# Projecting q, k and v of a slice in one place with full-size matmuls, in a four-layer attention and convolution kernel

## The chip, the cores and the metric

The kernel runs on one core of one Trainium2 chip. The metric is the device time of one execution in microseconds (us); the lower, the better. A core has a matmul engine (TensorE, PE in the profile; its weight loads are PEld), a vector engine (VectorE, DVE), an engine for functions and evictions (ScalarE, ACT), a general engine (GpSimd, POOL) and an engine that here only issues transfers (SyncE, SP).

## The reference

The input x is 4 images of 256 channels and 48 x 48 points, in float32. Four layers follow, each of the form x = x + layer(group norm of x):

- Layer 0: `qkv = w_qkv @ x`; q and k of each of 8 heads (64 channels) are divided by their norm over the 2304 points; `softmax(10 * q^T k)` weighs v; `w_out` projects the result.
- Layer 1: maximum pooling, a blur with stride 3, four depthwise convolutions of 11 x 3, a sigmoid gate that is spread back over the points and multiplies the layer's input.
- Layer 2: theta, phi and g project 256 channels to 64; `softmax(theta phi / 8)` over the 2304 points weighs g; `W` projects back to 256; a normalization over all images.
- Layer 3: a gate for each channel from the mean over the points, a depthwise 3 x 3 convolution, a normalization over the points and a leaky relu.

The change is in the projections of layers 0 and 2:

```python
qkv = jnp.einsum('oc,bchw->bohw', w_qkv, x)                    # layer 0
theta_x = jnp.einsum('oc,bcn->bno', theta_w, xt) + theta_b     # layer 2
phi_x = jnp.einsum('oc,bcn->bon', phi_w, xt) + phi_b[:, None]
g_x = jnp.einsum('oc,bcn->bno', g_w, xt) + g_b
```

## The kernel before

All four images stay in on-chip memory, as X[b], 128 partitions x 2 halves of the channels x 2304 points. The group norm is not applied to x: its scale goes into the weights (`norms`, L462) and its shift into a bias.

**Units, groups and slots.** Layer 0 goes through 16 phases, one for each image and pair of heads. A phase has six units (`l0_unit`, 384 query points each), and a unit has nine groups of two key blocks of 128 points. One group is one slot, so that a phase has 54. In a slot, `attend` writes out by hand, in this order: `scores` of the group (L239, quarter matmuls of 64x64, then exp on ACT into pt, L245), `add_up` of the group before (the sums for the softmax, on DVE into acc, L285, for some groups after a first addition on POOL into half, L270), what is due in the slot, the fills of the slot, the steps of layer 1 (`others`), and `weigh` of the group before (L259, into av). Every engine works through its own instructions in the order written. pt has five buffers, the PSUM tiles sc and pj two each.

**The end of a unit.** When its last group is weighed, in slot 0 of the next unit, `last` books: in slot 1 `total` (L292, the column sums of acc, into both pj tiles), in slot 4 `invert`, in slot 8 `divide`, and eleven slots later, in slot 2 of the unit after next, `out_proj`: two matmuls (L527) and two additions to X on DVE (L531).

**The next pair.** While a phase attends one pair of heads, it projects q, k and v of the next, slice by slice (384 points, read again from memory into xs, two buffers). `start` in slot 0 loads the weights w, `norms` in slot 2 scales them and makes a bias. `qk` stands in slots 4 and 6 of each unit: for each of two halves of the channels it issues four quarter matmuls (`quarters`, L226) into two pj tiles, one for each half of the rows, and `join` brings the first to q or k on ACT with the bias (L229), and adds the second on DVE (L230). Then ACT squares it for the norm (junk, L489). `values` (L497, full matmuls of 128x128) stands in slot 2 of the next unit, ahead of out_proj; the last slice's comes in the next phase (`late`). `scale` in slot 51 multiplies all of q (L518). For the first pair the same functions run one after another before `attend`.

**Layer 1 and layer 2.** Layer 1 of an image is cut into steps, mainly of DVE (L643 is its largest group), which run in the slots of the next image's phases. Image 0's phases have none. Layer 2 has three units for each image, of two column halves at once: kd holds phi twice, qv theta of one half of the points above theta of the other. `project2` of the next image is spread over slots, as phi (L703), theta (L714, one half of the columns in one call) and g (L727) for each slice; phi and theta are joined as q and k are. Layer 3 comes last.

In the hardware's count every float32 matmul is two instructions.

Of the kernel before, what the change touches and what calls it, by code (L numbers as in the profile page):

```python
# [9 lines left out]
F32 = mybir.dt.float32  # L10
# [4 lines left out]
P = 128  # L15
HW = 48
N = HW * HW
NK = 2
# [56 lines left out]
def usual_path(  # L75
# [146 lines left out]
    def quarters(outs, lhsT, rhs, start, stop):  # L222

        for c in HALVES:
            for r, out in zip(HALVES, outs):
                nc.tensor.matmul(out[c], lhsT=lhsT[r, c], rhs=rhs[r], start=start, stop=stop)  # L226

    def join(out, ab, bias):
        nc.scalar.activation(out, ab[0], AF.Identity, bias=bias)  # L229
        nc.vector.tensor_add(out, ab[1], out)  # L230

# [197 lines left out]
    def project(b, norm, pair):  # L429
# [9 lines left out]
        def start():  # L439
            at["w"] = wqp.tile([P, NK, 3, P], F32, tag="w", name="w")  # L440
            for k in range(NK):
                nc.sync.dma_start(at["w"][:, k], wqv[:, k, :, p * P : (p + 1) * P])
            fetch(0)
            pair["q"] = big.tile([P, N], F32, tag="q", name="q")
            pair["k"] = big.tile([P, N], F32, tag="k", name="k")
            pair["v"] = big.tile([P, JB, P], F32, tag="v", name="v")
            at["ss"] = small.tile([P, 2, NSL], F32, tag="ss", name="ss")

        def norms():

            w = at["w"]
            ps = pj_tile()
            for t in range(3):
                for k in range(NK):
                    nc.tensor.matmul(
                        ps[:, t : t + 1], lhsT=w[:, k, t, :], rhs=norm["nb"][:, k : k + 1],
                        start=k == 0, stop=k == NK - 1,
                    )
            at["bias"] = small.tile([P, 3], F32, tag="bias", name="bias")
            nc.vector.tensor_copy(at["bias"], ps[:, 0:3])  # L460
            for k in range(NK):
                nc.scalar.activation(  # L462
                    w[:, k], w[:, k], AF.Identity, scale=norm["rs"][:, k : k + 1]
                )
            fetch(1)
# [15 lines left out]
        def qk(s, t):  # L481
            cols = slice(s * SL, (s + 1) * SL)
            to = pair["qk"[t]]
            ab = [pj_tile()[:, :SL] for _ in range(2)]
            for k in range(NK):
                quarters(ab, at["w"][:, k, t, :], xs[s][:, k, :], k == 0, k == NK - 1)
            join(to[:, cols], ab, at["bias"][:, t : t + 1])
            junk = rpool.tile([P, SL], mybir.dt.bfloat16, tag="junk", name="junk")
            nc.scalar.activation(  # L489
                junk, to[:, cols], AF.Square, accum_out=at["ss"][:, t, s : s + 1]  # L490
            )

        def values(s):
            ps = pj_tile()
            for i in range(SL // P):
                for k in range(NK):
                    nc.tensor.matmul(  # L497
                        ps[:, i * P : (i + 1) * P], lhsT=xs[s][:, k, i * P : (i + 1) * P],
                        rhs=at["w"][:, k, 2, :], start=k == 0, stop=k == NK - 1,
                    )  # L500
            j0 = s * (SL // P)
            nc.scalar.copy(
                pair["v"][:, j0 : j0 + SL // P, :].rearrange("p j d -> p (j d)"), ps[:, :SL]
            )
            if s + 2 < NCH:
                fetch(s + 2)

        def scale():
# [9 lines left out]
            nc.vector.tensor_scalar(pair["q"], pair["q"], sc, None, ALU.mult)  # L518

        return start, norms, out_bias, qk, values, scale  # L520
# [149 lines left out]
    def project2(b, norm, s2):  # L670
# [3 lines left out]
        def start():  # L674
# [15 lines left out]
            w = wqp.tile([P, NK, 3, P], F32, tag="w", name="w2")  # L690
            for k in range(NK):
                nc.scalar.activation(
                    w[:, k, :, 0:D], w2c[:, k], AF.Identity, scale=norm["rs"][:, k : k + 1]
                )
            at["w"], at["bias"] = w, bias

        def phi(s):
            cols = slice(s * SL, (s + 1) * SL)
            ab = [pj_tile()[:, :SL] for _ in range(2)]
            for k in range(NK):  # L700
                for c in HALVES:
                    for r, out in zip(HALVES, ab):
                        nc.tensor.matmul(  # L703
                            out[c], lhsT=at["w"][r, k, 0, 0:D], rhs=X[b][r, k, cols],
                            start=k == 0, stop=k == NK - 1,
                        )
            join(s2["k"][:, cols], ab, at["bias"][:, 0:1])

        def theta(s):
            c, to = HALVES[s // L2C], (s % L2C) * SL  # L710
            ab = [pj_tile()[:, :SL] for _ in range(2)]
            for k in range(NK):
                for r, out in zip(HALVES, ab):
                    nc.tensor.matmul(  # L714
                        out[c], lhsT=at["w"][r, k, 1, 0:D],
                        rhs=X[b][r, k, s * SL : (s + 1) * SL],
                        start=k == 0, stop=k == NK - 1,
                    )
            join(s2["q"][c, to : to + SL], [half[c] for half in ab], at["bias"][c, 1:2])

        def g(s):
            ps = pj_tile()
            nj = SL // P
            for i in range(nj):
                for k in range(NK):
# [3 lines left out]
                        rhs=at["w"][:, k, 2, 0:D], start=k == 0, stop=k == NK - 1,  # L729
# [5 lines left out]

        return [start] + [
            (lambda fn=fn, s=s: fn(s)) for s in range(NCH) for fn in (phi, theta, g)
        ]

# [59 lines left out]
    order = [(b, p) for b in range(B) for p in range(NPAIR)]  # L799
    n = NCH * NG  # L800
    late = None
    for (b, p), after in zip(order, order[1:] + [None]):
        work, others = {}, []
        if late:
            work[2] = [late]
        if after:
            b1, p1 = after
            start, norms, out_bias, qk, values, scale = project(b1, norms0[b1], pairs[b1][p1])
            work.setdefault(0, []).append(start)
            work.setdefault(2, []).append(norms)  # L810
            work[NG + 2] = [out_bias]
            for s in range(NCH):
                for t, slot in ((0, 4), (1, 6)):
                    slot += NG * s - (s == NCH - 1)
                    work.setdefault(slot, []).append(lambda qk=qk, s=s, t=t: qk(s, t))
                if s + 1 < NCH:
                    work.setdefault(NG * (s + 1) + 2, []).append(lambda v=values, s=s: v(s))
            work.setdefault(n - 3, []).append(scale)
            late = lambda v=values: v(NCH - 1)
# [35 lines left out]

    _drain(gn(0, norms0[0]))
    start, norms, out_bias, qk, values, scale = project(0, norms0[0], pairs[0][0])
    start()
    norms()
    for s in range(NCH):  # L860
        for t in range(2):
            qk(s, t)
        values(s)
    scale()
    out_bias()
# [1128 lines left out]
```

## Time and profile before

| | |
|---|---|
| median of 3 runs | 3950.24 us (3950.04 to 3954.59) |
| the profiled execution | 3949.85 us, span 3948.0 us |
| PE busy | 3614.1 us, 92% |
| DVE busy | 2939.9 us, 74% |
| ACT busy | 2089.8 us, 53% |
| POOL busy | 1449.4 us, 37% |
| first scores of layer 0 | 70.29 us after the span's start |
| layer 0 to about 3140 us, layer 2 to about 3660 us, then layer 3 | |

The page gives the busy time of each engine, the same in 40 slices of 98.7 us as tenths, and groups of equal instructions with their mean duration. An engine's idle time is put down to the instruction that ended it (`<-`). Matmuls overlap, so that the time from one start to the next, which the timeline shows, is what a matmul costs in a row, and its own duration (485 ns here) is longer. The quarter matmuls run four at a time.

### The profile page before, as it was taken

How to read it: one execution, taken by the hardware profiler on the slowest of the kernel's cores; microseconds unless marked ns; L12 is line 12 of the kernel's file. 1: busy time of each engine (PE TensorE's matmuls, PEld its weight loads, DVE VectorE, ACT ScalarE, POOL GpSimd, SP SyncE). 2: the span in 40 equal slices, each digit the busy share in tenths (PEclk: the TensorE clock that was granted, in tenths of full speed). 3: DMA queues.
4: the chain of work that ended last, by engine and by line, in shares of the span. 5: the costliest groups of instructions: out<-in, count | busy, mean ns of one | idle time of the engine just before them, and what ended most of it. 6: DMA issues, size and time to landing. Idle time of an engine off the chain costs nothing.

```text
span 3948.0 us, 91093 instructions
## 1 busy us (share of the span) xinstructions
PE 3614.1 (92%) x38738; PEld 1751.8 (44%) x38738; DVE 2939.9 (74%) x3733; ACT 2089.8 (53%) x3226; POOL 1449.4 (37%) x858
## 2 busy tenths in 40 slices
PE   6999999999999999999999999999999988779785
PEld 3444444444444444444444444444444444334343
DVE  2566555678987896789878967897788678856477
ACT  3666656655555555565565555655655544334222
POOL 1333333333333333333433333334334355443232
PEclk9999999999999999999999999999999999889787
DMA  4111111111111111111111111111110000000001
GB/s 148 24 25 21 24 20 29 24 20 24 20 24 20 24 20 24 24 24 20 21 20 26 20 24 20 24 20 23 21 13 8 6 5 5 5 5 4 0 36 61
DMA packets 109439, 91.09 MB, mean 23 GB/s; under 512 B 56048, under 2 KB 106848, under 8 KB 107104
## 3 DMA queue, kind: packets, MB, share of 16 engines
q1 hardware_dynamic: 106256, 84.06, 12.0%
q8 instruction: 305, 5.00, 0.5%
q10 hardware_dynamic: 2768, 1.14, 0.1%
q14 instruction: 110, 0.90, 0.1%
HBM read 54.62 MB, written 9.44 MB: 16 GB/s over the span
## 4 chain that ended last, share of the span: by engine, by line
PE 57%; DVE 30%; issue 5%; ACT 4%; POOL 3%; DMA 1%; SPq 0%; DVEq 0%; ACTq 0%; POOLq 0%
PE av L259 19%; PE sc L239 18%; DVE acc L285 14%; DVE l1acc L643 6%; PE pj L226 6%; PE pj L527 3%; PE pj L497 3%; PE sc L1028 3%; PE pj L292 2%; POOL half L270 1%; ACT pt L245 1%; DVE gn_st L168 1%; ACT k L229 1%; DVE k L230 1%; DVE z L1043 1%
## 5 line engine op out<-in xcount | busy, mean ns | idle before, releaser
L245 ACT ACTIVATE pt<-sc 128x768 f32<-128x768 f32 x1944 | 1482.4, 809 | 1096.2 <-PE sc L239 934.9
L270 POOL TENSOR_TENSOR half<-pt 128x768 f32<-128x768 f32 x477 | 977.5, 2050 | 2105.4 <-ACT pt L245 1893.6
L239 PE MATMUL sc<-q,k 64*64 64x384 f32 x13824 | 1288.6, 485 | 17.7 <-ACT pt L245 15.2
L259 PE MATMUL av<-pt,v 64*64 64x384 f32 x13824 | 1299.9, 489 | 4.7 <-ACT raw L328 4.7
L285 DVE TENSOR_TENSOR acc<-acc,pt 128x768 f32<-128x768 f32 x792 | 943.9, 1192 | 62.5 <-ACT pt L245 1.9
L239 PEld LDWEIGHTS sc<-q,k 64*64 64x64 f32 x13824 | 527.2, 134 | 625.8 <-issue 523.0
L259 PEld LDWEIGHTS av<-pt,v 64*64 64x64 f32 x13824 | 522.0, 134 | 611.3 <-issue 596.0
L285 DVE TENSOR_TENSOR acc<-acc,half 128x768 f32<-128x768 f32 x459 | 480.7, 1047 | 68.7 <-POOL half L270 65.7
L643 DVE SCALAR_TENSOR_TENSOR l1acc<-pd,grid,l1acc 128x256 f32<-128x256 f32 x640 | 464.4, 726 | 16.3
L531 DVE SCALAR_TENSOR_TENSOR x<-pj,bo,x 128x384 f32<-128x384 f32 x192 | 118.5, 618 | 263.3 <-PE pj L527 262.9
L226 PE MATMUL pj<-xs,w 64*64 64x384 f32 x3072 | 290.7, 485 | 5.7 <-ACT q L229 4.1
L239 PE MATMUL sc<-qv,kd 64*64 64x384 f32 x1728 | 188.8, 504 | 18.3 <-ACT pt L245 18.2
L259 PE MATMUL av<-pt,qv 64*64 64x384 f32 x1728 | 197.7, 522 | 6.3 <-ACT raw L328 6.3
L292 PE MATMUL pj<-acc,ones 64*64 64x384 f32 x832 | 98.4, 534 | 99.5 <-DVE acc L285 98.6
L1028 PE MATMUL sc<-pad,diag 128*128 128x384 f32 x480 | 173.4, 516 | 11.9 <-ACT pad L1006 11.9
L226 PEld LDWEIGHTS pj<-xs,w 64*64 64x64 f32 x3072 | 118.3, 133 | 142.5 <-issue 125.7
L527 PE MATMUL pj<-o,wo 128*128 128x384 f32 x384 | 158.9, 518 | 16.7 <-DVE bias L460 11.1
L497 PEld LDWEIGHTS pj<-w,xs 128*128 128x128 f32 x1152 | 135.9, 191 | 53.5 <-issue 42.8
L497 PE MATMUL pj<-w,xs 128*128 128x128 f32 x1152 | 153.8, 283 | 4.0 <-ACT k L229 4.0
L230 DVE TENSOR_TENSOR k<-pj,k 128x384 f32<-128x384 f32 x96 | 53.4, 556 | 138.1 <-ACT k L229 136.1
L336 POOL TENSOR_TENSOR o<-o,rinv 128x384 f32<-128x384 f32 x95 | 138.9, 1462 | 0.0
L230 DVE TENSOR_TENSOR q<-pj,q 128x384 f32<-128x384 f32 x96 | 53.5, 557 | 112.0 <-ACT q L229 112.0
(190 smaller groups left out, 2654.3 us busy)
## 6 DMA issues: line engine op xcount, KB each, us to landing
xs<-in_x_dram SPq DMA_DIRECT2D x96, 384.0 KB, 3.2
rinv<-rinv SPq DMA_DIRECT2D x208, 94.5 KB
x<-in_x_dram SPq DMA_DIRECT2D x8, 1152.0 KB, 5.4
out_dram<-x SPq DMA_DIRECT2D x7, 1152.0 KB, 4.2
l<-row SPq DMA_DIRECT2D x416, 1.5 KB, 1.8
w<-in_wqkv_dram SPq DMA_DIRECT2D x32, 192.0 KB, 6.7
rinv<-ls SPq DMA_DIRECT2D x208, 1.5 KB, 1.8
out_dram<-x SPq DMA_DIRECT2D x2, 576.0 KB, 3.3
```

The costliest lines, as they stand in the source:

```text
L226: nc.tensor.matmul(out[c], lhsT=lhsT[r, c], rhs=rhs[r], start=start, stop=stop)
L230: nc.vector.tensor_add(out, ab[1], out)
L239: nc.tensor.matmul(ps[c * D : (c + 1) * D, h, :SL], lhsT=u["of"]["k"][r, j0 : j0 + D], rhs=u["of"]["q"][r, u["qc"]], start=True, stop=True,)
L245: nc.scalar.activation(pt, ps[:, :, :SL], AF.Exp, scale=u["scale"])
L259: nc.tensor.matmul(u["av"][h * D : (h + 1) * D, half, :SL], lhsT=value(u, j, h)[r], rhs=pt[r, h, :], start=j == 0, stop=j == JB - 1,)
L270: nc.gpsimd.tensor_add(half, pts[0], pts[1])
L285: nc.vector.tensor_add(u["acc"], u["acc"], term)
L292: nc.tensor.matmul(out[c], lhsT=ones[r], rhs=u["acc"][r, h, :], start=True, stop=True)
L497: nc.tensor.matmul(ps[:, i * P : (i + 1) * P], lhsT=xs[s][:, k, i * P : (i + 1) * P], rhs=at["w"][:, k, 2, :], start=k == 0, stop=k == NK - 1,
L527: nc.tensor.matmul(ps[:, :SL], lhsT=wo[:, p, k * P : (k + 1) * P], rhs=o, start=True, stop=True)
L643: nc.vector.scalar_tensor_tensor(acc, src, w, acc, ALU.mult, ALU.add)
L1028: nc.tensor.matmul(self.ps[:, s % 2, :SL].rearrange("p (r c) -> p r c", c=HW), lhsT=diag[:, self.k, PE_TAPS.index(t), :], rhs=self.pad[:, ...
```

## The change

q, k and v of a slice are now made by one function, `chunk`, in slot 2 of each unit, ahead of out_proj: `values`, then q, then k. q and k are full matmuls, 128 rows and 128 columns, accumulated over the two halves of the channels in one pj tile; ACT brings them to q and k with the bias, and DVE has no part in it. `quarters` and `join` are gone. The weights are loaded half a phase earlier (`prefetch`, slot 27 of the phase before) and scaled in slot 47 of the phase before (`norms`), `start` reads the first two slices, `scale` multiplies q in three parts in slots 51 to 53, and nothing is late. In layer 2 phi's weights are stored twice, side by side, so that one full matmul gives both copies of kd; theta makes both halves of the columns in one call, as two matmuls of 128 rows and 64 columns, in three calls and not six.

```diff
-    def quarters(outs, lhsT, rhs, start, stop):
-
-        for c in HALVES:
-            for r, out in zip(HALVES, outs):
-                nc.tensor.matmul(out[c], lhsT=lhsT[r, c], rhs=rhs[r], start=start, stop=stop)
-
-    def join(out, ab, bias):
-        nc.scalar.activation(out, ab[0], AF.Identity, bias=bias)
-        nc.vector.tensor_add(out, ab[1], out)
...
-        def start():
+        def prefetch():
             at["w"] = wqp.tile([P, NK, 3, P], F32, tag="w", name="w")
             for k in range(NK):
                 nc.sync.dma_start(at["w"][:, k], wqv[:, k, :, p * P : (p + 1) * P])
-            fetch(0)
-            pair["q"] = big.tile([P, N], F32, tag="q", name="q")
...
+        def start():
+            pair["q"] = big.tile([P, N], F32, tag="q", name="q")
...
+            fetch(0)
             fetch(1)
...
         def qk(s, t):
             cols = slice(s * SL, (s + 1) * SL)
-            to = pair["qk"[t]]
-            ab = [pj_tile()[:, :SL] for _ in range(2)]
+            to = pair["qk"[t]][:, cols]
+            ps = pj_tile()[:, :SL]
             for k in range(NK):
-                quarters(ab, at["w"][:, k, t, :], xs[s][:, k, :], k == 0, k == NK - 1)
-            join(to[:, cols], ab, at["bias"][:, t : t + 1])
+                nc.tensor.matmul(
+                    ps, lhsT=at["w"][:, k, t, :], rhs=xs[s][:, k, :],
+                    start=k == 0, stop=k == NK - 1,
+                )
+            nc.scalar.activation(to, ps, AF.Identity, bias=at["bias"][:, t : t + 1])
...
+        def chunk(s):
+            values(s)
+            for t in range(2):
+                qk(s, t)
             if s + 2 < NCH:
                 fetch(s + 2)
...
-            nc.vector.tensor_scalar(pair["q"], pair["q"], sc, None, ALU.mult)
+            at["sc"] = sc
+            rescale(0)
+
+        def rescale(i):
+            q = pair["q"][:, i * 2 * SL : (i + 1) * 2 * SL]
+            nc.vector.tensor_scalar(q, q, at["sc"], None, ALU.mult)
...
         def phi(s):
+
             cols = slice(s * SL, (s + 1) * SL)
-            ab = [pj_tile()[:, :SL] for _ in range(2)]
+            ps = pj_tile()[:, :SL]
             for k in range(NK):
...
+                nc.tensor.matmul(
+                    ps, lhsT=at["w"][:, k, 0:2, :].rearrange("p t d -> p (t d)"),
+                    rhs=X[b][:, k, cols], start=k == 0, stop=k == NK - 1,
+                )
+            nc.scalar.activation(
+                s2["k"][:, cols], ps, AF.Identity, bias=at["bias"][:, 0:1]
+            )
 
         def theta(s):
...
+            ps = pj_tile()[:, :SL]
             for k in range(NK):
-                for r, out in zip(HALVES, ab):
+                for i, c in enumerate(HALVES):
+                    s0 = (s + i * L2C) * SL
                     nc.tensor.matmul(
...
+                        ps[c], lhsT=at["w"][:, k, 2, :], rhs=X[b][:, k, s0 : s0 + SL],
                         start=k == 0, stop=k == NK - 1,
                     )
...
+            new = projs[i + 1]
+            work[0] = [new["start"]]
             for s in range(NCH):
...
+                work[NG * s + AT_CHUNK] = [lambda new=new, s=s: new["chunk"](s)]
+            work[NG + AT_CHUNK].append(new["out_bias"])
+            for j, fn in enumerate(new["scale"]):
+                work[n - 3 + j] = [fn]
+            if i + 2 < len(order):
+                work[n // 2] = [projs[i + 2]["prefetch"]]
+                work[NG * (NCH - 1) + AT_CHUNK].append(projs[i + 2]["norms"])
```

## The prediction, made before the changed kernel ran

> **What bounds the kernel now.** I read first the slices of the page, then windows of busy time, then the waits of VectorE (DVE) and TensorE (PE), then the timeline of the start and of one unit. The slices:
>
> ```profile
> PE   6999999999999999999999999999999988779785
> DVE  2566555678987896789878967897788678856477
> ```
>
> PE is full from slice 2 to about 32, and not in the first or in layer 2 and 3. DVE rises and falls: low while image 0 is attended, high where layer 1 of an earlier image rides along. Two windows (sum, then PE, PEld, DVE, ACT, POOL, clock, DMA) give sizes:
>
> ```profile
> 400.00:700.00 300.00, 298.60 (x3457) 146.39 (x3450) 175.41 (x223) 180.15 (x282) 101.55 (x63) 1.00 0.15 24
> 1000.00:1300.00 300.00, 280.26 (x3156) 132.93 (x3152) 253.99 (x311) 169.76 (x271) 113.81 (x63) 0.98 0.13 21
> ```
>
> In the first PE idles 1.4 us of 300, in the second 19.7, with DVE at 85%. Who waits:
>
> ```profile
> DVE x L531 <- PE pj L527: 262.9, 172, 7.0
> DVE k L230 <- ACT k L229: 136.1, 60, 3.6
> DVE q L230 <- ACT q L229: 112.0, 88, 5.1
> PE pj L292 <- DVE acc L285: 98.6, 65, 6.5
> ```
>
> The last is what DVE costs PE: at the end of a unit the sums of acc are late and total (L292) waits. The first is DVE waiting for the output projection, in the middle of its own queue. One unit shows both:
>
> ```profile
> 1015.25 0.88 PE L292 MATMUL pj<-acc,ones 64*64 64x384 f32 x8 [1.40 <-DVE acc L285]
> 1019.11 1.58 PE L497 MATMUL pj<-w,xs 128*128 128x128 f32 x12
> 1020.53 1.64 PE L527 MATMUL pj<-o,wo 128*128 128x384 f32 x4
> 1021.38 0.62 DVE L531 SCALAR_TENSOR_TENSOR x<-pj,bo,x 128x384 f32<-128x384 f32 x1 [1.57 <-PE pj L527]
> ```
>
> From total to total a unit takes 29.6 us with image 0, which is PE's own work, and 31 to 35 us with layer 1 beside it. So there the loop is: acc done, PE to the output projection, DVE from there to the next acc. The start is a chain of single steps:
>
> ```profile
> 34.25 0.58 ACT L229 ACTIVATE q<-pj,bias 128x384 f32<-128x384 f32 x1 [1.61 <-PE pj L226]
> 34.86 0.56 DVE L230 TENSOR_TENSOR q<-pj,q 128x384 f32<-128x384 f32 x1 [3.80 <-ACT q L229]
> 34.88 2.11 PE L226 MATMUL pj<-xs,w 64*64 64x384 f32 x16 [0.68 <-ACT q L229]
> ```
>
> Both pj buffers belong to one q or k, so PE stops for each: 7.14 us a slice (L226 at 32.05 and 39.20), first scores at 70.29.
>
> **What the Trainium skill says.** "TensorEngine Tiling (Array Packing)", Key Properties: a change of tiling mode drains TensorE. The trace agrees: starts of matmul groups are 0.32 us apart inside one mode, 0.41 to 0.42 at a change. "TensorE: Matmul & The Clock Gate", queue depths under its architectural detail: ScalarE and VectorE are strict first-in first-out. The waits at L531 agree: additions ready behind it don't overtake. "SBUF — State Buffer", shared port: a DVE instruction with two SBUF inputs and a GpSimd one exclude each other. The trace agrees in size: an acc addition takes 0.95 us alone and up to 2.5 us beside half (2.05 us).
>
> **The change, part by part.**
>
> (1) *Full instead of quarter matmuls for q and k.* Sixteen quarter instructions (L226, 1002.07 to the next group at 1003.36) take 1.29 us of PE. Four full ones: L1028, the same 128x384 shape, issues 20 in 6.72 us, (6.72 - 0.485)/19 = 0.33 us each, 1.3 us. Its weight loads (0.19 us) hide behind that. So nothing changes: 0. Price if they didn't hide: L527 also shows 0.43 us; 4 x 0.1 x 192 = 80 us, taken as a tail only. Layer 2's phi is the same exchange, eight quarters for two full ones in a slice; its doubled weights are two small copies on ScalarE (ACT, busy 53%) ahead of the first use. Mode changes stay one pair a unit, because chunk sits in slot 2 with out_proj, where values were.
>
> (2) *No joins.* 96 q and 96 k at 0.556 us: 107 us less on DVE, 1.11 us a unit. The 0.62 us for which ACT waits before each junk goes too. Only beside layer 1 is DVE late, so for image 0 I take 0 (PE's 29.6 us hide it).
>
> (3) *chunk ahead of out_proj.* q and k were at slots 4 and 6; now 2 x 1.29 = 2.58 us stand in slot 2 ahead of out_proj, whose result L531 waits for in DVE's queue. Behind L531 stand the unit's layer 1 step and four rounds of acc additions. From total to the first L531 is 5.7 us in most units; it becomes 8.3, while DVE comes there at 4.4. PE has 2.58 us less to do afterwards, so the loop gains 2.58 of wait and loses 1.11 of joins and 0.35 of their wait: about +1.1 us where DVE is busy all the way, and I add 0.1 for additions that fall beside half. By the unit-to-unit timeline that holds in about 36 units; in 28 others with layer 1 DVE waits for q or k anyway, so the late end is set by PE's slots: -1.0 to +0.8, I take -0.3. 36 x 1.2 - 28 x 0.3 = **+35 us**. Bounds: 0 (the waits at L230 were all on the path) and +96 (64 x 1.5, none was).
>
> (4) *Start.* A slice is 1.34 us of values and 2.58 of q and k, 3.94 with the mode alike; ACT needs 0.48 + 2 x (0.58 + 0.71), 3.1, and each pj tile is free before PE returns to it. Six: 23.6 from 24.2, so 47.8. Then k's eviction and square 1.5, the scale chain 1.5, a third of the q rescale (1.42/3) 0.5: scores at 51.3, 19.0 earlier. Given back: x of images 1 to 3 (6 x 1152 KB) is issued at about 41 and moves at the 421 GB/s of before's 60 to 65 us, until 57.5; xs of the next pair stands behind it on SP's queue and lands at about 59.5, while chunk in slot 2 wants it at 57.2. Net **-16.5** (-19 to -12).
>
> (5) *Prefetch, norms, rescale.* w comes half a phase early, norms moves to slot 47, behind chunk and ahead of out_proj; the same 12 matmuls and the same copy by DVE ahead of L531. SP's order changes only by DMAs that wait for nothing late. In the last unit the sums of squares are ready four slots before scale (L510 and L515 waited 1.5 us). Chunk makes out_proj's second tile wait for k's eviction by 0.1 us. On ACT the chunk queues three evictions and two squares, 3.1 us, between the exps of slots 2 and 3; PE needs 6.5 us from the first to the second (1.34 + 2.58 + 1.3 + 1.29 of L259), so the exps aren't late; the cover is gone if an exp of slot 2 itself waits over 1 us for DVE to free its pt, and then out_proj waits for both. The xs reads of a slice are issued behind chunk and wanted nine slots later, so their 3.2 us are hidden; v of the new pair is first written in slot 2 and not in slot 11, after the last reading of the old one in slot 0. **-1** (-6 to +6).
>
> (6) *Last phase of layer 0.* project2 for image 0: theta halves. L714's eight instructions use two of four quarters, 1.29 us a slice for six slices; after, three calls of 1.29, if two 128x64 tiles run together, which L344 shows (pairs start 6 ns apart). -3.9 on PE; 12 joins leave DVE, and no chunk is added here: **-9** (-12 to -3).
>
> (7) *Layer 2.* In 3200 to 3400 DVE is busy 171.5 of 200 us and PE 161.6, so DVE's 24 joins (kd, qv, 13.3 us) and 4 of their waits come off the path: -16. In image 2's last unit (about 3497 to 3570) project2 is a chain as at the start: PE waits 0.8 for ACT kd in each slice, 4 for DVE kd, 1.6 more, and theta's 3.9: -12. **-28** (-40 to -15).
>
> Sum against the profiled execution, 3949.85 us (span 3948.0 and 1.85 around it): +35 - 16.5 - 1 - 9 - 28 = -19.5, **3930 us**. The median of the runs is 3950.24, 0.4 above it, so they stand for the same.
>
> **Rivals.** A change of 0.2%, 8 us, is about what a measurement here can tell.
>
> *L531 blocks more than the joins free* (slower). Mechanism as in (3), in all 64 units at 1.5 us: +96 - 54.5 = +41, **3991 us**. For it: DVE comes to L531 at 4.4 us, so it would sit idle for 4 us a unit; heavy layer 1 steps and half can't be moved into that hole. Against: 28 units had waits at L230 of 1.6 us and more. It decides once the mean loss passes 54.5/64 = 0.85 us a unit, and is over 0.2% from 0.97.
>
> *DVE's relief is paid in full* (faster). The waits at L230 (248 us) were on the path, so (3) is 0: **3895 us**. For it: the chain of waits runs through L230 beside layer 1. Against: where DVE is late, that wait is only 0.35 us.
>
> *The full matmuls issue at 0.43 us*: +80 us, about 4010. Against it stand 20 in a row at 0.33.
>
> **How the numbers follow.** Forecast 0.50 (its own range 3905 to 3955), L531 slower 0.31, relief in full 0.15, slow issue 0.04. The forecast's cases fall 0.37 faster, 0.10 same, 0.03 slower; the relief's are all faster; those of L531 start near the break-even, 0.03 of them within 0.2%. Faster 0.52, same 0.13, slower 0.35. The range, 3885 to 3990, reaches to both first rivals.
>
> **What will show it.** First scores near 51 us. q and k without DVE; PE L478 at 1.3 us for four. DVE's wait at out_proj's addition up from 263 us to over 450; units beside layer 1 at 32 to 36 us, PE's wait for acc at total up from 99 us to 120 or more. Three calls of theta at 1.3 us. Layer 2 ended 28 us sooner after its start. If the wait at the addition stays at 263 us, (3) is wrong; if total's wait falls, the relief won; if units grow by over 1 us on the mean, the first rival has.

## The result and the profile after

The changed kernel takes **3969.5 us** (median of 4 runs, 3967.5 to 3976.9) where the kernel before takes 3950.1 on the same chip: a ratio of 1.0050, with a 95% interval of 1.0032 to 1.0067. It is half a per cent slower; 3930 us, faster, was forecast. The profiled execution is the longest of the four runs, 3976.9 us with a span of 3975.0, 7.4 us above the median, so the two profiles are 27 us apart and not 19: the differences between their stages below carry up to 7 us that the other executions did not have.

The slices of the changed kernel's page (busy tenths of PE and DVE):

```profile
PE   7999999999899999999899999998999997879785
DVE  2565555568888787678787876887878769966477
```

PE is fuller at the start and emptier while layer 1 rides along: slices 11, 20 and 28 fall to 8, while DVE there is mostly below what it was. Neither engine is busier there, and the kernel is slower. The same two windows as before (length, then busy us of PE, PEld, DVE, ACT, POOL, granted clock, DMA share, GB/s):

```profile
400.00:700.00 300.00, 296.44 (x3210) 147.42 (x3210) 169.65 (x208) 178.98 (x279) 96.88 (x63) 1.00 0.15 25
1000.00:1300.00 300.00, 272.42 (x2813) 132.20 (x2806) 240.89 (x278) 165.77 (x262) 109.23 (x61) 0.98 0.13 21
```

In the second, PE idles 27.6 us of 300 (19.7 before) and DVE has 13 us less to do. Both wait more. The waits say for what (total us, times, longest):

```profile
DVE x L539 <- PE pj L535: 398.2, 153, 9.1
...
ACT pt L235 <- DVE acc L275: 154.3, 152, 4.4
...
PE pj L282 <- DVE acc L275: 127.0, 63, 7.5
...
DVE bias L445 <- PE pj L440: 99.1, 15, 10.0
...
DVE bo L470 <- PE pj L462: 72.7, 12, 8.4
```

The addition of out_proj (L539, L531 before) waits 398 us and not 263, total 127 and not 99. The copies of the norms' bias and of bo, which stand behind the chunk as well, wait 172 us together (69.7 before). The 248 us of waits at the joins are gone with them; the new waits at these three places, 237 us, nearly fill their place. Exp (L235) waits 154 us for acc to give back a pt tile, where it waited 46. The unit shown of the kernel before at 1015.25 is this one now (timeline of the changed kernel, PE and DVE):

```profile
1016.07 0.88 PE L282 MATMUL pj<-acc,ones 64*64 64x384 f32 x8 [1.74 <-DVE acc L275]
...
1019.46 1.60 PE L492 MATMUL pj<-w,xs 128*128 128x128 f32 x12
...
1020.90 2.75 PE L478 MATMUL pj<-xs,w 128*128 128x384 f32 x8
1023.48 0.50 PE L462 MATMUL pj<-bias,wo 128*128 128x1 f32 x4
1024.02 0.16 DVE L470 COPY bo<-pj 128x2 f32<-128x2 f32 x1 [3.46 <-PE pj L462]
1024.33 1.53 PE L535 MATMUL pj<-o,wo 128*128 128x384 f32 x4 [0.34 <-DVE bo L470]
1025.25 1.26 DVE L539 SCALAR_TENSOR_TENSOR x<-pj,bo,x 128x384 f32<-128x384 f32 x2 [1.07 <-PE pj L535]
```

From total to the addition it was 6.1 us; it is 9.2, and DVE stands idle for 3.46 + 1.07 us of it. The start is shorter: first scores at 53.12 us, not 70.29. But:

```profile
53.12 1.52 PE L229 MATMUL sc<-q,k 64*64 64x384 f32 x16 [1.17 <-DVE q L523]
...
65.50 2.90 PE L492 MATMUL pj<-w,xs 128*128 128x128 f32 x12 [6.42 <-DMA xs<-in_x_dram]
```

The first chunk of the loop waits 6.42 us for its xs, and PE's next starts are at half pace (12 instructions of L492 took 1.6 us above and take 2.9 here). The clock that was granted to TensorE, in the column before the last two, is 0.50 there:

```profile
65.50:68.50 3.00, 3.00 (x13) 3.00 (x14) 0.00 (x0) 0.06 (x1) 0.00 (x0) 0.50 0.06 18
```

For everything that follows the span is cut at the totals into six stages, worked out from the starts of total (first of its eight matmuls): to the first total; image 0 (24 units); the 65 units beside layer 1; the last phase of layer 0, up to the first total of layer 2; layer 2, up to its last total; the rest.

| profile of | start | image 0 | beside layer 1 | last phase | layer 2 | rest |
|---|---|---|---|---|---|---|
| before | 100.9 | 720.7 | 2116.2 | 226.0 | 406.7 | 377.5 |
| changed | 91.8 | 725.6 | 2181.1 | 221.0 | 375.7 | 379.9 |
| difference | -9.1 | +4.9 | **+64.9** | -5.0 | **-31.0** | +2.4 |

By the place of a unit in its phase, the 65 units split. The four kinds of unit without the phase's last chunk (44 units) lost 34.6 us together, 0.8 us each. The 11 that hold the last chunk, norms and scale lost 35.5 us, 3.2 us each; the remaining 10, which begin a phase and held norms in the kernel before, gained 5.3 together.

One thing differs between executions as well. In image 0 the granted clock never falls. Beside layer 1 the trace's record of it has stretches at 0.50, each 3.4 or 6.8 us long, and in these two profiles each follows an idle gap of PE of 1.9 to 4.8 us: 14 stretches, 54.6 us, before, and 16, 71.7 us, in the changed kernel. At half the clock PE does half its work, so a stretch costs at most half its length, and by this estimate at most 9 of the 64.9 us are the clock's. The waits come first.

### The profile page after: what moved, and what is told of

It reads as the page before. It is cut to its first block, busy times and chain, and to the rows that moved or that the text cites. A ratio compares the mean times of both kernels' runs of the same rounds, so it can differ in the third digit from the quotient of the medians.

```text
span 3975.0 us, 85528 instructions
## 1 busy us (share of the span) xinstructions
PE 3601.6 (91%) x36050; PEld 1764.9 (44%) x36050; DVE 2862.1 (72%) x3525; ACT 2092.1 (53%) x3222; POOL 1421.2 (36%) x858
## 4 chain that ended last, share of the span: by engine, by line
PE 50%; DVE 39%; issue 5%; ACT 3%; POOL 2%; DMA 1%; DVEq 0%; SPq 0%; ACTq 0%; POOLq 0%
DVE acc L275 21%; PE av L249 15%; PE sc L229 14%; DVE l1acc L651 8%; PE pj L478 6%; PE pj L535 4%; PE pj L492 3%; PE sc L1041 3%; PE pj L282 2%; ACT pt L235 1%; DVE z L1056 1%; DVE x L675 1%; DVE gn_st L168 1%; DVE lsum L312 1%; PE pj L740 1%
## 5 line engine op out<-in xcount | busy, mean ns | idle before, releaser
L235 ACT ACTIVATE pt<-sc 128x768 f32<-128x768 f32 x1944 | 1492.4, 810 | 1263.7 <-PE sc L229 1000.4
L260 POOL TENSOR_TENSOR half<-pt 128x768 f32<-128x768 f32 x477 | 952.5, 1998 | 2173.8 <-ACT pt L235 1710.3
L275 DVE TENSOR_TENSOR acc<-acc,pt 128x768 f32<-128x768 f32 x792 | 970.4, 1225 | 86.4 <-DVE acc L275 3.2
L275 DVE TENSOR_TENSOR acc<-acc,half 128x768 f32<-128x768 f32 x459 | 497.7, 1084 | 166.3 <-POOL half L260 163.9
L651 DVE SCALAR_TENSOR_TENSOR l1acc<-pd,grid,l1acc 128x256 f32<-128x256 f32 x640 | 451.7, 706 | 16.2
L539 DVE SCALAR_TENSOR_TENSOR x<-pj,bo,x 128x384 f32<-128x384 f32 x192 | 118.3, 617 | 399.1 <-PE pj L535 398.2
L478 PE MATMUL pj<-xs,w 128*128 128x384 f32 x768 | 268.1, 490 | 9.9 <-ACT v L497 9.9
L229 PE MATMUL sc<-qv,kd 64*64 64x384 f32 x1728 | 177.4, 506 | 23.9 <-ACT pt L235 23.7
L249 PE MATMUL av<-pt,qv 64*64 64x384 f32 x1728 | 179.3, 515 | 7.1 <-ACT raw L318 7.1
L478 PEld LDWEIGHTS pj<-xs,w 128*128 128x128 f32 x768 | 138.8, 192 | 89.8 <-ACT v L497 15.4
L492 PEld LDWEIGHTS pj<-w,xs 128*128 128x128 f32 x1152 | 138.7, 194 | 63.8 <-issue 57.8
L492 PE MATMUL pj<-w,xs 128*128 128x128 f32 x1152 | 156.3, 286 | 8.0 <-DMA xs<-in_x_dram 6.4
L1041 PEld LDWEIGHTS sc<-pad,diag 128*128 128x128 f32 x480 | 94.6, 203 | 86.1 <-issue 22.3
L287 ACT COPY row<-pj 128x384 f32<-128x384 f32 x208 | 89.9, 490 | 63.9 <-PE pj L282 63.9
```

The lines of the kernel that those rows point to most:

```text
L229: nc.tensor.matmul(ps[c * D : (c + 1) * D, h, :SL], lhsT=u["of"]["k"][r, j0 : j0 + D], rhs=u["of"]["q"][r, u["qc"]], start=True, stop=True,)
L235: nc.scalar.activation(pt, ps[:, :, :SL], AF.Exp, scale=u["scale"])
L249: nc.tensor.matmul(u["av"][h * D : (h + 1) * D, half, :SL], lhsT=value(u, j, h)[r], rhs=pt[r, h, :], start=j == 0, stop=j == JB - 1,)
L260: nc.gpsimd.tensor_add(half, pts[0], pts[1])
L275: nc.vector.tensor_add(u["acc"], u["acc"], term)
L478: nc.tensor.matmul(ps, lhsT=at["w"][:, k, t, :], rhs=xs[s][:, k, :], start=k == 0, stop=k == NK - 1,)
```

## The experiments

Three theories were tried. **QUEUE**: DVE takes its instructions in order, so whatever of PE stands ahead of out_proj holds DVE up at its addition. **CROWD**: norms, scale and the last chunk in one unit are what costs. **BURST**: a whole chunk in one slot, with three evictions and two squares of ACT behind it, stops scores and exp, in whatever order. (The texts count 18 passes; the timeline above has 20 instructions, 12 of L492 and 8 of L478.) Every time below is a median, and each ratio is to runs of the kernel before on the same chip (medians of 3952.5 to 3955.1 us).

### Layer 2 alone

The kernel before, with the changed `project2` only. In phi and in theta alike:

```diff
-            ab = [pj_tile()[:, :SL] for _ in range(2)]
+            ps = pj_tile()[:, :SL]
...
```

> The kernel before with only the new layer 2 projection (phi doubled, theta in column halves); layers 0 and 1 keep their quarters, joins and places. If the parts of the change are independent, the 31 us that layer 2 lost between the two profiles (406.7 to 375.7 us) appear alone: 3919 us, 3914 to 3926, all of it between the first and the last total of layer 2. Rival: layer 2 was shorter only because the changed layer 0 left other work or a different clock behind it; then less than half of it appears, 3935 or more.

Measured: **3919.2 us**, ratio 0.9917 (0.9900 to 0.9933). Layer 2's stage is 376.5 us, 30.2 less, and image 0 and the 65 units stay as they were (720.7 and 2114.4). This half of the change is independent and worth 33 us. So the other half, the one in layers 0 and 1, costs some 50 us on top of it.

### The order in slot 2

First out_proj alone goes ahead of the chunk (a table `ahead` that `attend` empties before the fills), then out_bias and norms too:

```diff
-        todo += [(fills, after, fn) for fn in u["after"]]
+        todo += [(ahead, after, fn) for fn in u["after"]]
...
             do(due, t)
+            do(ahead, t)
             do(fills, t)
```

> The changed kernel with out_proj issued ahead of the chunk in slot 2, all else as it is. Theory QUEUE (VectorE's in-order queue stands at out_proj's addition until the chunk of 18 passes is through TensorE): VectorE's wait at that addition falls from 398 us to under 100, the waits of exp for pt and of total for acc fall with it, and 35 to 50 of the 65 us lost beside layer 1 come back: 3920 to 3935. Theory CROWD (norms, three pieces of scale and the last chunk of a phase meet in one unit): these stay where they are, 0 to -5 us: 3965 to 3970. Theory BURST (18 passes and five evictions in one slot stop scores and exp, whatever their order): the same 3965 to 3972, or slower where the chunk now waits for the addition to free its tiles.

```diff
-            work[NG + AT_CHUNK].append(new["out_bias"])
+            work[NG + AT_CHUNK].insert(0, new["out_bias"])
...
-                work[NG * (NCH - 1) + AT_CHUNK].append(projs[i + 2]["norms"])
+                work[NG * (NCH - 1) + AT_CHUNK].insert(0, projs[i + 2]["norms"])
```

> As the run with out_proj ahead, and in the second unit out_bias, in the last unit norms are also issued ahead of the chunk, so that the two small VectorE copies behind them do not wait for the chunk. QUEUE: the wait at the copy of the norms' bias falls from 99 us to under 30, the one at bo from 73 to under 25, and the unit from the last chunk, 3.2 us longer in each phase beside layer 1, comes down: a further 15 to 30 us, 3895 to 3915. CROWD: that unit still holds norms and scale, so it stays some 3 us longer in each phase: no more than 5 us below the run with out_proj ahead. BURST: 3965 to 3972.

Measured: **3902.5 us** (0.9872; 0.9856 to 0.9889) and **3887.5 us** (0.9835; 0.9818 to 0.9851). The first takes 70.3 us out of the 65 units, more than QUEUE expected, and no instruction is added or taken away. The waits of out_proj ahead alone:

```profile
DVE x L541 <- PE pj L537: 184.3, 60, 5.0
...
PE pj L282 <- DVE acc L275: 97.6, 66, 7.5
...
DVE bias L447 <- PE pj L442: 71.1, 15, 5.0
```

The wait at the addition is halved (not under 100, as expected) and total's is back at 98. BURST and CROWD alone both expected 3965 or more and are out as the main cause. The second takes another 21.7 us out of the 65 units, 10.2 of it in those with the last chunk, and lies below QUEUE's range too.

### How much may stand in front

Out_bias and norms ahead of the chunk in all four; out_proj ahead of the chunk (above), behind the values (1.3 us of PE), behind values and q (2.6), behind the whole chunk (3.9):

```diff
-        todo += [(fills, after, fn) for fn in u["after"]]
+        for fn in u["after"]:
+            fns = fills.setdefault(t + after, [])
+            fns.insert(max(0, len(fns) - 1), fn)
...
-                work[NG * s + AT_CHUNK] = [lambda new=new, s=s: new["chunk"](s)]
+                work[NG * s + AT_CHUNK] = [lambda new=new, s=s: new["values"](s), lambda new=new, s=s: new["both"](s)]
```

So `fills` puts out_proj between the two; for the next version the parts are values with q, and k. In these texts g1 is the version with the whole chunk ahead of out_proj, the third below.

> The version with out_bias and norms ahead of the chunk, with out_proj between the values and the full passes of q and k: 1.3 of the chunk's 3.9 us stand ahead of it, where the changed kernel has 3.9 and the version with all ahead none. If the time lost grows with what is in front: a third of the 67 us between these two, 3910, 3902 to 3920. If only a whole chunk in front is too much: 3884 to 3893. If any work ahead costs nearly as much as the chunk: 3930 to 3955.

> As the run with out_proj between values and q, but between q and k: 2.6 of the chunk's 3.9 us stand ahead of it. With 1.3 us it took 3879. GRADUAL (from 1.3 us on each further us costs the same): half way from there to g1, 3905 to 3922. LATE THRESHOLD (only the last 1.3 us are too much): 3879 to 3890. EARLY THRESHOLD: 3935 or more.

> The changed kernel with norms and out_bias ahead of the chunk; out_proj stays behind it. If the two shares add up, what these two gave when out_proj was already ahead (15 us by the medians, 22 in the profiles) comes off here too: 3945 to 3956, nearly all of it in the unit from the last chunk, while the four units between stay some 0.8 us longer than before. If VectorE stands at out_proj's addition anyway, so that its earlier copies gain nothing: 3963 to 3970.

Measured: **3879.2**, **3912.0** and **3964.6 us** (ratios 0.9812, 0.9895 and 1.0032, each within 0.002). The first is below all that was expected of it; the second is where GRADUAL expected it. One line of waits from each, in this order:

```profile
DVE x L540 <- PE pj L536: 259.6, 172, 5.6
```

```profile
DVE x L543 <- PE pj L539: 378.6, 177, 8.1
```

```profile
DVE x L539 <- PE pj L535: 490.8, 182, 8.2
```

The means over the 44 units without a last chunk, worked out from the timeline (us from total):

| PE ahead of out_proj | addition starts | DVE waits for it | acc addition, mean | unit | run |
|---|---|---|---|---|---|
| 0 | 4.67 | 1.25 | 1.05 | 31.48 | 3887.5 |
| 1.3 | 5.97 | 2.04 | 1.07 | 31.54 | 3879.2 |
| 2.6 | 7.42 | 3.48 | 1.17 | 32.33 | 3912.0 |
| 3.9 | 8.61 | 4.66 | 1.26 | 33.03 | 3964.6 |

In these units the first 1.3 us are free: when out_proj goes first, the values wait for the addition to give back a pj tile, and the block is through PE at the same time (9.7 and 9.6 us after total). From there on 2.62 us more of DVE's wait make a unit 1.49 us longer. So the loss is gradual, and over half of the wait reaches the unit's end.

The 8 us between 3887.5 and 3879.2 come from elsewhere, from the ten intervals in which a phase begins (334.0 to 320.1 us; those with the last chunk give 4 back). In the second of the ten a long step of layer 1 stands ahead of the addition in DVE's queue, and with out_proj first the whole chunk waits for it (timeline with all ahead):

```profile
1173.99 5.11 DVE L677 TENSOR_TENSOR x<-x,l1acc 128x768 f32<-128x768 f32 x3
...
1183.14 2.52 PE L494 MATMUL pj<-w,xs 128*128 128x128 f32 x12 [4.06 <-DVE x L541]
```

In the ten together PE waits 22 us at the values; with the values first it waits 11, at out_proj.

The acc additions also become dearer on the mean, by 0.19 us each from 1.3 to 3.9 us ahead, 13 in a unit. The traces show what decides it. In these units of six profiles (before, changed and the four of the table) an addition with no GpSimd instruction beside it takes 0.95 to 0.96 us on the mean, and one that overlaps with such an instruction 1.36 to 1.55, up to 2.6. Of 13 in a unit, 3.2 overlap with 1.3 us ahead and 6.8 with 3.9. The Trainium skill, "SBUF — State Buffer", under who interferes with whom, says that a DVE instruction with two SBUF inputs contends with a GpSimd one that reads SBUF; the traces agree. But layer 1's accumulations into l1acc (0.48 us alone, 1.4 beside GpSimd) meet it less often instead, 1.2 and not 3.1 a unit, so that DVE's busy time in a unit grows by only 0.8 us in all.

The last of the three runs also refutes the expectation that norms' order is worth 15 us by itself: with out_proj still behind the chunk it gives 5 (3969.5 to 3964.6), which the intervals of the two ratios don't separate from nothing. DVE, spared at the copy, waits at the addition instead (491 us there).

### Norms in another unit

```diff
-                work[NG * (NCH - 1) + AT_CHUNK].insert(0, projs[i + 2]["norms"])
+                work[NG * 4 + 6] = [projs[i + 2]["norms"]]
```

> The same version with the norms of the next pair's weights in slot 42, a unit ahead of the last chunk and the scale. CROWD (the unit from the last chunk holds norms, the scale chain and the chunk, and is the one type that is still longer than before, by 1.0 us beside layer 1 and 2.3 us in image 0): 10 to 20 us less, 3868 to 3878. QUEUE alone: what norms cost only moves to another unit, 3884 to 3890.

Measured: **3889.6 us**, no gain over 3887.5. The 11 intervals with the last chunk fall from 370.1 to 358.9 us, and those one unit earlier rise from 346.9 to 361.7. Norms cost about a microsecond wherever they are; CROWD falls.

### The passes at their old places

The version with all ahead, with q and k at slots 4 and 6 again (full passes):

```diff
+                for t in range(2):
+                    slot = NG * s + 4 + 2 * t - (s == NCH - 1)
+                    work[slot] = work.get(slot, []) + [lambda new=new, s=s, t=t: new["qk"](s, t)]
```

> The same version with the full passes of q and k at the old slots 4 and 6, the values alone in slot 2. QUEUE: once out_proj is ahead, where the passes stand counts little, 3880 to 3895. BURST (18 passes in a row stop scores and exp for some 5 us, and the halves of the clock that follow): 10 to 25 us less, 3862 to 3877. Two more changes of the array's mode a unit, were they dear (0.2 us and more), would give 3905 to 3920.

Measured: **3870.3 us** (0.9789; 0.9773 to 0.9806). BURST has its share: the 65 units are 26.5 us shorter (2089.1 to 2062.6), 12.5 of it in those with the last chunk. Stretches at half the clock fall from 37.5 to 23.9 us with it, worth 7 us at most. But image 0 is 13.1 us longer. Then the same only beside layer 1, with image 0 left in one place (`if b == 0`, the loop keeps `chunk`):

> The version with out_proj, out_bias and norms ahead of the chunk; while image 0 is at work (TensorE has no slack there) q, k and values stay in one place, beside layer 1 q and k go to slots 4 and 6. If image 0's 13 us in the spread version are the price of the array's further mode changes where TensorE sets the time, they come back: 3857, 3852 to 3863. If the first image was longer for another reason (evictions of q and k at those slots), 3866 to 3872.

Measured: **3859.6 us** (0.9761; 0.9745 to 0.9777), with image 0 at 726.6 and the 65 units at 2062.2. So in this kernel one place is right where PE sets the time and wrong where DVE does.

### The change without its moves

The kernel before with the new layer 2, and q and k as full passes without joins; everything else of layers 0 and 1 where it was:

```diff
-            ab = [pj_tile()[:, :SL] for _ in range(2)]
+            ps = pj_tile()[:, :SL]
             for k in range(NK):
-                quarters(ab, at["w"][:, k, t, :], xs[s][:, k, :], k == 0, k == NK - 1)
-            join(to[:, cols], ab, at["bias"][:, t : t + 1])
+                nc.tensor.matmul(
+                    ps, lhsT=at["w"][:, k, t, :], rhs=xs[s][:, k, :],
+                    start=k == 0, stop=k == NK - 1,
+                )
+            nc.scalar.activation(
+                to[:, cols], ps, AF.Identity, bias=at["bias"][:, t : t + 1]
+            )
```

> The kernel before with the new layer 2 projection and q and k in full passes without joins, but everything of layers 0 and 1 at its old place: values and then out_proj in slot 2, q in slot 4, k in slot 6, late values, no weights ahead. It is the change without its moves. QUEUE (the moves put 3.9 us of TensorE ahead of VectorE's addition; with 1.3 us ahead, as here, little is lost): the joins' 1.11 us a unit come off wholly or in part, 3860 to 3895, some 25 to 60 below the run with layer 2 alone. MODE (full passes among the quarters at three places cost more than they save): 3915 or more.

Measured: **3865.2 us** (0.9775; 0.9759 to 0.9791), 54 us below layer 2 alone and 104 below the full change. Its window beside layer 1:

```profile
1000.00:1300.00 300.00, 292.89 (x3032) 138.21 (x3034) 244.19 (x309) 175.32 (x281) 105.55 (x64) 0.99 0.14 21
```

PE idles 7.1 us of 300, not 27.6. The 65 units take 2055.2 us, 59.2 less than with layer 2 alone: 0.91 us a unit, against the 1.11 that the joins took. At most 15 of the 59 are the clock's (51.2 us at half the clock in the one, 20.5 in the other). So the new arithmetic is worth 54 us, and the new places cost about twice that. Image 0 is 15.5 us longer here (13.1 in the spread version): in its timeline PE goes from scores to q in 0.413 us and from q to av in 0.416, where quarters among quarters took 0.303. Two blocks of full passes more in each unit make four such changes, 0.11 us each, which is 10.6 of the 15.5 us in 24 units; the rest stays open.

### The order without the change, and the place with the joins

The kernel before with out_proj ahead of its values, and the version with all ahead with quarters and joins put back into its chunk:

> The kernel before with out_proj ahead of the values in slot 2, nothing else. QUEUE: its VectorE also stands at out_proj's addition, 263 us in all, behind 1.34 us of values; the wait falls under 150 and 10 to 30 us come off: 3920 to 3940. If the order matters only where a whole chunk is in front: within 4 us, 3947 to 3955.

> The version with out_proj, out_bias and norms ahead of the chunk, with q and k projected again in quarters into two tiles and joined on VectorE, at the new place. Theory PAID IN FULL (with the queue unblocked, the 1.11 us of VectorE a unit that the joins took are all on the path beside layer 1): 65 units by 1.1 us and up to 20 more in the start and image 0: 3950 to 3975. Theory IN PART (a third to a half of it is on the path, the rest lies beside other work): 3915 to 3935. Theory HIDDEN: 3885 to 3895, and then what the order gives is all that there is.

Measured: **3974.2 us** (1.0054; 1.0038 to 1.0071) and **4230.2 us** (1.0699; 1.0681 to 1.0717). Both miss every expectation. In the first the wait only moves to the next instruction of DVE's queue that wants PE and ACT:

```profile
DVE q L230 <- ACT q L229: 343.1, 96, 5.3
...
DVE x L533 <- PE pj L529: 170.2, 59, 5.7
```

263 us have become 170 at the addition, and q's join has gone from 112 to 343. That by itself is no loss: 55 of the 65 units are together 4 us shorter. The ten in which a phase begins are 19.5 us longer (329.6 to 349.1). There the values wait for the addition, and behind the values stand norms, for whose copy DVE then waits in turn (the second of the ten):

```profile
1197.55 2.61 PE L499 MATMUL pj<-w,xs 128*128 128x128 f32 x12 [4.07 <-DVE x L533]
...
1202.55 0.16 DVE L462 COPY bias<-pj 128x3 f32<-128x3 f32 x1 [4.53 <-PE pj L457]
```

In the second both joins of a slice follow each other in DVE's queue, each behind PE and ACT (timeline of that run):

```profile
1035.34 0.58 ACT L230 ACTIVATE q<-pj,bias 128x384 f32<-128x384 f32 x1 [1.61 <-PE pj L227]
1035.95 0.56 DVE L231 TENSOR_TENSOR q<-pj,q 128x384 f32<-128x384 f32 x1 [3.98 <-ACT q L230]
...
1038.73 0.56 DVE L231 TENSOR_TENSOR k<-pj,k 128x384 f32<-128x384 f32 x1 [2.22 <-ACT k L230]
```

DVE idles 6.2 us in this slice, PE stops between q and k because both pj tiles belong to q, and image 0 (778 us, +52) and the 65 units (2366, +277) both pay. A single place for q and k is bearable only because the joins are gone: full passes leave nothing there for DVE to wait for, and take one pj tile each.

### The start

The changed kernel with the loads of images 1 to 3 in slots 15, 24 and 33 of the first phase, and the same on the version spread beside layer 1:

```diff
+        if i == 0:
+            for b1 in range(1, B):
+                work.setdefault(6 + NG * b1, []).append(lambda b1=b1: load_x(b1))
...
-    for b in range(1, B):
-        load_x(b)
     attend(phases)
```

> The changed kernel with the loads of images 1 to 3 issued in the first phase (slots 15, 24 and 33), not ahead of it. If the first chunk's xs waits behind these loads on the way to memory and the unit after it pays with the half clock, some 7 us come back: 3962, 3958 to 3966, with the first unit shorter by that. Rival: the wait is for the two fetches themselves, 0 to -2 us: 3967 to 3970.

> The same with the loads of images 1 to 3 in slots 15, 24 and 33 of the first phase. Only the start gains: 5 us below the run beside it. If the 14 us that beside layer 1 were also shorter in the earlier run with later loads belong to the loads, 12 to 18 us below it.

Measured: **3957.8 us** (1.0014; 1.0006 to 1.0023), 11.7 below the changed kernel, and **3852.4 us**, 7.2 below its neighbour. In both the start is shorter, by 4.9 and 7.0 us. The other 7 us of the first run lie beside layer 1, as the profile has it too (2167.3, against 2181.1); the second run has no such gain (2062.1 and 2062.2). The loads explain the start: in both timelines the first chunk now follows the scores with no wait for xs. Why those units were also shorter in the first run stays open; its profile has 41.0 us at half the clock there against 71.7, which is worth 15 us at most.

### What the findings point to

Spread beside layer 1, one place for image 0, out_bias and norms ahead, loads later, and out_proj behind the values again:

```diff
-            do(ahead, t)
             do(fills, t)
```

`fills` then runs out_bias or norms, the values and out_proj, in this order.

> The version spread beside layer 1 with the loads of x in the first phase, with out_proj behind the values again instead of ahead of them. With out_proj ahead the values' first tile waits for VectorE's addition; with 1.3 us ahead nothing was lost. So 4 to 9 us below 3852: 3840 to 3849. If it is the same, 3850 to 3855, the order of these two does not matter here.

Measured: **3844.4 us** (0.9728; 0.9711 to 0.9744), 2.7% faster than before and 3.2% faster than the change as it was made. Its 65 units take 2054.7 us, as in the change without its moves; image 0 takes 725.0 and the start 86.4. The 8 us that it is below the run before it (3852.4) come from the ten intervals at the beginning of a phase again (331.2 to 318.6; those with the last chunk give 5 back). At half the clock it spends 6.8 us beside layer 1.

## Why the prediction was wrong

The profile's 27 us against the sum of the steps:

| step | forecast | measured |
|---|---|---|
| (1) full passes | 0 | 0.323 us a pass, 0.33 was taken |
| (3) chunk ahead of out_proj, with (2) | +35 | +34.6 in the 44 units without a last chunk |
| (5) prefetch, norms, rescale | -1 | +30.2 in the other 21 units, +4.9 in image 0 |
| (4) start | -16.5 | -9.1 |
| (6) last phase of layer 0 | -9 | -5.0 |
| (7) layer 2 | -28 | -31.0 |
| rest | 0 | +2.4 |

This table divides by unit. The runs divide the 65 units by cause as well, if they are put in a row (each difference is to the line above):

| 65 units beside layer 1 | us | difference |
|---|---|---|
| layer 2 alone, with quarters and joins | 2114.4 | |
| the changed kernel | 2181.1 | +66.7 |
| out_proj ahead of the chunk | 2110.8 | -70.3 |
| out_bias and norms ahead too | 2089.1 | -21.7 |
| q and k at their old slots | 2062.6 | -26.5 |
| the change without its moves, with out_proj behind the values | 2055.2 | -7.4 |

In another order the shares differ: with norms and out_bias ahead first, out_proj ahead takes 77.8 us off (2166.9 to 2089.1).

**The step that failed most is (5).** It put norms and the chunk's length at next to nothing. It took norms to be "the same 12 matmuls and the same copy by DVE ahead of L531", and no more, and it checked the chunk against ACT's exps but the unit with the last chunk not against DVE. There norms, the chunk and out_proj stand in one slot, so 1.4 us of norms and 3.9 of chunk are ahead of the addition, and three pieces of scale follow for DVE. These intervals went from 358.8 to 394.3 us. Part of that loss is out_proj's wait, which step (3) had reckoned for 64 units, these among them: with out_proj ahead they take 380.3. Out_bias and norms ahead bring them to 370.1, and with the passes spread as well they are at 357 to 358, where they were before. Over all 65 units what the step put at -1 is worth 21.7 us for the copies behind the chunk and 26.5 us for the passes in one place; whether these 26.5 come by late scores or late exps was not separated. The forecast's bound of +6 for this step was the one too narrow.

**Step (3) had the mechanism, but not its shape, and its sum is in part luck.** The addition was to start 2.6 us later after total; it starts 2.7 later (6.16 to 8.88 on the mean of the 44). DVE's busy time in these units falls by 1.07 us, the joins' 1.11. But the +34.6 of the table are 44 units, and the forecast's +35 were for 64. By cause, the order of out_proj costs 70.3 us and the joins give back 59.2, +11 net. And the 28 units that were to gain 0.3 each, because "DVE waits for q or k anyway", are not found: only 16 of the 65 are shorter, 9 of them units that begin a phase, and all four kinds of unit without a last chunk are longer on the mean, by 0.2 to 1.2 us. The two gross terms were larger than the step's net lets one see: the joins' removal alone takes 59 us off the 65 units, the moves put 126 back (2055.2 to 2181.1), of which the clock can be 26 at most (20.5 and 71.7 us at half of it). As a net of two large numbers +35 was fragile, and its upper bound of +96 was the honest part. The additions had been given 0.1 us a unit for falling beside half; against before the 13 are 0.04 us dearer each (1.22 to 1.26), 0.5 us a unit.

**Step (4) was sized wrong at its second term.** The first scores came at 53.1 us (51.3 was worked out). But xs was to land 2.3 us after it was wanted; PE waited 6.42 us and went on at half the clock, and of 17.2 us gained, 8 were given back. The loads of images 1 to 3 ahead of it are the cause: moved away, they give 5 to 7 us.

**Steps (1), (2), (6) and (7).** Full passes in a row start 0.323 us apart (L478; 0.33 was taken), so the rival at 0.43 us is out. Step (6) is right in sign and short by half. Step (7) is right, and the run with layer 2 alone confirms it by itself.

**The rivals.** "L531 blocks more than the joins free" came nearest: it asked for over 0.85 us a unit, and the 65 units lost 1.0 on the mean. But it gave them 1.5 alike, for L531 alone; the 44 lost 0.8, and the last-chunk units, for reasons that it didn't name, 3.2. "DVE's relief is paid in full" was near about the relief, 0.91 us of 1.11, and wrong that nothing would take it away again. Of the two signs that were to tell them apart, total's wait went from 99 to 127, as the forecast asked. The wait at the addition rose to 398 us, not over 450; with the two copies behind the same chunk it is from 333 to 570.

## What to carry to other kernels

Before moving work of one engine, list what stands behind it in the queues of the others: here the change added no work, but 2.6 us of matmuls in front of one instruction that VectorE waits for cost 85 us. Judge a faster operation and its new place apart, one run for each; the operation was worth 54 us, and the places took 104. And judge a place by stage: passes in one block are best where TensorE sets the time, spread ones where it waits for VectorE; and out_proj first was worse than second just where VectorE came late to it.

## What the runs showed of the hardware

- A float32 pass of 128x384 (one instruction; a matmul has two) starts 0.323 us after the one before it, four quarters of 64x384 together in the same 0.32. A change between the two costs 0.11 us each way (0.413 and 0.416 against 0.303).
- After a wait of 6.42 us, PE's granted clock was 0.50 until 68.58 us, and its next 12 instructions took 2.9 us, not 1.6. Beside layer 1, in the profiles before and after, each stretch at 0.50 lasted 3.4 or 6.8 us and followed an idle gap of PE of 1.9 to 4.8 us.
- The same acc addition took 0.95 us with no GpSimd instruction beside it, and 1.36 to 1.55 us on the mean, up to 2.6, with one.
